# Two-layer convolution and local attention on 8 images: the position map kept in DRAM, the emptying of the queries moved, and inverse roots by Ln and Exp

## The chip, the cores and the metric

The kernel runs on one core of a Trainium2 chip. The metric is the device time of one execution in microseconds (us). A core has TensorE (PE in the profile) for matmuls, VectorE (DVE), ScalarE (ACT) and GpSimd (POOL) for the rest, and SyncE (SP), which here only issues DMAs. "PEld" is TensorE's loading of weights, listed apart from the matmuls. "SPq" and "ACTq" are DMA issues by these two engines.

## The reference

Eight images of 256 channels and 64 x 64 pixels, in float32, go through two residual layers. Both begin with a group norm over 32 groups of 8 channels. Cut to what matters:

```python
def layer0(x):                       # x is group-normed
    x1, x2, x3 = conv1x1(x, w1), conv1x1(x, w2), conv1x1(x, w3)   # 32, 32, 256 channels
    h = concat(x1, unfold3x3(reflect_pad(x2)))                    # 320 channels
    h = relu(bn(h)); h = relu(bn(conv1x1(h, cw1)))                # 32 channels
    w = conv1x1(h, cw2) + cb2                                     # 9 weights per pixel and group
    return sum over the 9 taps of unfold3x3(zero_pad(x3)) * w

def layer1(x):                       # x is group-normed
    pe = Wp @ position(64, 64) + bp  # the position map: depends on neither the image nor x
    q, k, v = conv1x1(x, Wq) * 64 ** -0.5, conv1x1(x, Wk), conv1x1(x, Wv)     # 4 heads of 64
    att = softmax over 7x7 neighbours of q . unfold7x7(reflect_pad(k) + reflect_pad(pe))
    out_att = sum over neighbours of att * unfold7x7(reflect_pad(v))
    wts = softmax over 9 branches of conv1x1(x, Wfc)
    hid = relu(depthwise3x3(x, w1))  # one per branch, with the branch's own kernels
    out_conv = sum over branches of depthwise3x3(hid, w2) * wts
    return rate1 * out_att + rate2 * out_conv

x = x + layer0(group_norm(x))
x = x + layer1(group_norm(x))
```

`group_norm` divides by sqrt(variance + eps); this inverse root is one of the things the change rewrites.

## The kernel before

**Tiling.** An image is cut into NB = 8 bands of R = 8 rows (512 pixels). Channels lie on the 128 partitions, in two tiles (`ct` = 0, 1). The main loop (line 1032) counts bands with `g`, from -12 to 63; `b, i = divmod(g, 8)` are image and band. Layer 1 of band `g` is worked on while layer 0 of band `g + 12` is prepared beside it, because layer 1's group norm needs the whole of layer 0's image first. In the loop's first 12 rounds layer 0 runs alone ("alone" in the code). A band has STEPS = 8 steps (`s`): four pairs of 8 x 8 query tiles for each `ct`, `m` = 0 to 3.

**One step.** Scores go from TensorE (L736, `sco`) to DVE, which adds the mask and takes the negated maximum (L750, `nmax`). ACT takes the exponentials and sums them (L758, `prob` and `tot`). DVE inverts `tot` (L765) and ACT scales (L767). One step later TensorE transposes the probabilities (L773, `ptp`), ACT copies them out (L775), and TensorE multiplies them with the values (L785). Beside this stand, in each step, two matmul groups of the branch weights (L872, `pf`, four 128x512 matmuls with their weights), each with an exponential on ACT (L877, `ex`), the depthwise convolutions on DVE (L829, L855), the sum over the branches on POOL and DVE (L1087, L885 to L899), and the taps of layer 0: TensorE makes their weights (L464, `pw`), DVE multiplies (L477, `prod`), POOL adds up (L485, `xg`).

**Order of work.** The whole order is written out by hand: nothing is reordered, and each engine executes its instructions in the order in which the Python code emits them. `advance()` ends a place in this order, and `after(n, f)` runs `f` n places later. `beside(g, s)` gives three lists of extra work for a step: `head`, `mid`, `end`. A function in `head` or `mid` issues its matmuls when called and may return a second function, called one place later, which empties PSUM. `steer` adds the loads and the group norms. The order around `head` is:

```python
prob, nmax = masked(nm, m, sco)
...
    tot = exponentials(nm, prob, nmax)
ahead = [f() for f in head]
advance()
for f in ahead:
    if f:
        f()
```

**What the change touches.**

- *Queries* (L662 to L677): two matmuls per `ct` into `pq`, and at once, in the same function, an ACTIVATE that writes the scaled result into `qb` (L674). In most bands the queries stand in `mid`. In an image's first band the second half stands in `head` of step 3 and in its last band too, and the first half of such a band in `head` of step 7 of the band before. There ACT's `qb` comes behind the exponentials of the same step. `keys` in `head` of step 7 of other bands return their emptying as a second function, so their order stays.
- *Position map* (L643 to L652): for the rows of keys that are new in a band, POOL adds a column vector `pecol` and a row vector `perow` into one tile `pe` with a single buffer. It is called from `mid` in step 5 of the band before, or in step 4 if the coming band is an image's first or last. The first band of an image has 11 new rows (352 KB), the middle ones 8 (256 KB), the last 5 (160 KB). Its readers are DVE's `keys` (L700 and L707), which add it to the keys in `kb`. POOL also copies the six old rows of `kb` (L660).
- *Inverse roots* in `gn_affine` (L225 to L272), with `sc_a` for layer 0's norm and `sc_b` for layer 1's: two small matmuls `pg` (L237) form means over groups, then come variance plus eps (L258, DVE), square root (L262, ACT), reciprocal (L266, DVE), spread over fixed numbers of places. `rstd_` (L143 to L146) does the same once for the two batch norms. ACT's functions stand in table sets, and a change of the set is an instruction of its own (ACT_TABLE_LOAD); the compiler inserts it, at the line of the ACTIVATE that needs it.

**Queues.** SP issues nearly all DMAs, in order: a DMA that waits for something holds all later ones. For a band it issues the stores of the values `vd` (L614, L618, L625), the loads of value tiles `vt` (L636), the rows of layer 1's input `yp` (L557 to L561), the residual `xr` (L1000), and for layer 0 `xc`, `xs`, `xg`, `x3q` and the stores of `x` (L376, L523). ACT normalises `yp` in place (L566) when it has landed. The constants are loaded by ACT's queue at the start (L109).

**PSUM.** The pool tag "gen" has four buffers, which `pq`, `pk`, `pf`, `pw`, `ptp`, `pv` (L594), `p3` (`p` in the profile, L369), `pg` and others share in turn. A matmul group therefore starts only when the group four before it has been emptied, and TensorE's waits are named after whichever engine empties late.

Of the kernel before, what the change touches and what calls it, by code (L numbers as in the profile page):

```python
# [10 lines left out]
F32 = mybir.dt.float32  # L11
BF16 = mybir.dt.bfloat16
AF = mybir.ActivationFunctionType
# [5 lines left out]
P = 128  # L19
# [36 lines left out]
CHUNK = R * KW  # L56
NPROB = 2 * CHUNK
NEG = -1.0e30


AHEAD = NB + 4
# [25 lines left out]
def conv_layers_kernel(ctx: ExitStack, tc: tile.TileContext, ins: dict, out: bass.AP):  # L87
    nc = tc.nc
# [18 lines left out]
    def load(name, shape, src=None, now=True):  # L107
        t = const.tile(shape, F32, name=f"c_{name}")
        late.append(lambda: nc.scalar.dma_start(out=t, in_=ins[name] if src is None else src))  # L109
        if now:  # L110
            late.pop()()
        return t

    gmat = load("gmat", [P, P])
    par = load("par", [P, NPAR])
    chan = load("chan", [P, NCT, NCHAN], ins["chan"].rearrange("(t p) n -> p t n", p=P))
# [23 lines left out]
    for t in probs + x3n + h2n:  # L140
        nc.gpsimd.memset(t, 0.0)

    def rstd_(out_, var, eps):  # L143
        nc.vector.tensor_scalar(out_, var, eps, None, ALU.add)
        nc.scalar.activation(out_, out_, AF.Sqrt)
        nc.vector.reciprocal(out_, out_)  # L146


    bn1s = const.tile([P, 3], F32, name="bn1s")
# [34 lines left out]
    dram = ctx.enter_context(tc.tile_pool(name="dram", bufs=3 * NB, space=DRAM))  # L184
# [40 lines left out]
    def gn_affine(sts, means, name, done):  # L225


        n = len(sts)
        mv = stat.tile([P, n, 2], F32, name=f"mv_{name}", tag=f"mv{n}")
        for ct, st in enumerate(sts):  # L230
            nc.vector.bn_aggr(mv[:, ct, :], st)
        mean, var = mv[:, :, 0], mv[:, :, 1]
        gm, d, sc, bi = (stat.tile([P, n], F32, name=f"{v}_{name}", tag=f"{v}{n}") for v in ("gm", "d", "sc", "bi"))

        def group_means(v, k):
            pg = ps.tile([P, n], F32, name=f"pg_{name}_{k}", tag="gen", bufs=4)
            nc.tensor.matmul(pg, means, v, start=True, stop=True)  # L237
            return pg


        def a1():
            pg = group_means(mean, 0)
            after(2, lambda: a2(pg))

        def a2(pg):
            nc.vector.tensor_copy(gm, pg)
            for ct in range(n):
                c = slice(ct, ct + 1)
                nc.vector.tensor_scalar(d[:, c], pg[:, c], mean[:, c], None, ALU.subtract)
                nc.vector.tensor_scalar(d[:, c], d[:, c], d[:, c], var[:, c], ALU.mult, ALU.add)  # L250
            after(5, a3)

        def a3():
            pg = group_means(d, 1)
            after(2, lambda: a4(pg))

        def a4(pg):
            nc.vector.tensor_scalar(sc, pg, GN_EPS, None, ALU.add)  # L258
            after(2, a5)

        def a5():
            nc.scalar.activation(sc, sc, AF.Sqrt)  # L262
            after(4, a6)

        def a6():
            nc.vector.reciprocal(sc, sc)  # L266
            for ct in range(n):
                c = slice(ct, ct + 1)
                nc.vector.tensor_scalar(bi[:, c], gm[:, c], sc[:, c], -1.0, ALU.mult, ALU.mult)
            done(sc, bi)  # L270

        after(3, a1)  # L272
# [370 lines left out]
    def position(b, i):  # L643

        first, last = new_keys(i)
        n, a = last - first, i * R + first
        pe = images[b].pe[i] = w1.tile([P, KW - PAD, W], F32, tag="pe", name=f"pe_{b}_{i}", bufs=1)
        nc.gpsimd.tensor_add(
            pe[:, :n],
            pecol.unsqueeze(1).to_broadcast([P, n, W]),  # L650
            perow[:, a : a + n].unsqueeze(2).to_broadcast([P, n, W]),
        )  # L652

    def key_block(b, i, ct):

# [354 lines left out]
    with tc.manual_schedule():  # L1010

        for i, use in enumerate(("xc", "xc", "xr", "xr", "xs", None, None, None)):
            t = None
            if use is None:
                t = w1.tile([P, NCT, RP, W], F32, tag="yp", name=f"x_{i}", bufs=3)
                t = t.rearrange("p t r c -> p t (r c)")[:, :, :BAND]
            x = first_stats(0, i, use, t)
            if use == "xc":
                images[0].xc[i] = x
            advance()  # L1020
        for r in range(NB, AHEAD0 - AHEAD):
            first_stats(*divmod(r, NB))
        for _ in range(10):
            advance()
        scaled_weights(0)
        for _ in range(32):
            advance()
        for n, f in enumerate(layer1_loads()):
            after(4 * STEPS * (3 + n), f)

        pending, before, conv, convs = [], None, None, []
        for g in range(-AHEAD, B * NB):
            b, i = divmod(g, NB)
            for s in range(STEPS):
                ct, m = divmod(s, NT // 2)
                head, mid, end = beside(g, s)
                steer(g, s)
                if g >= 0:
                    nm = f"{b}_{i}_{ct}_{m}"
                    weighted = []  # L1040
                    if m % 2 == 0:
                        sco = score_tile(nm)
                        for e in range(2):
                            scores(b, i, ct, m + e, sco)
                        small = small_tile(nm)
                        weighted, pending = weigh_steps(pending, small), []
                        if s == 0 and g + AHEAD < B * NB:
                            mid.append(small_maps(*divmod(g + AHEAD, NB), small))
                        if s in (4, 6) and convs:
                            convs.pop()(small)  # L1050
                        if before is not None:
                            pending.append((before[:-1], transposed(nm, before[-1])))
                    prob, nmax = masked(nm, m, sco)
                    for a, po in weighted:
                        add_values(*a, po)
                    tot = exponentials(nm, prob, nmax)
                ahead = [f() for f in head]
                advance()
                for f in ahead:
                    if f:  # L1060
                        f()
                if g >= 0:
                    ex, exb = w1.tile([P, 2, BAND], F32, tag="ex", name=f"ex_{nm}", bufs=3), ex if m else None
                    branch_weights(b, i, ct, m, 0, ex)
                    if m % 2:
                        pending.append((before[:-1], transposed(nm, before[-1])))
                    if m in (0, 2):
                        todo = list(conv[0])
                    for _ in range(2):
                        todo.pop(0)()  # L1070
                advance()
                if g >= 0:
                    probabilities(prob, tot)
                rest = [f() for f in mid]
                advance()
                for f in rest:
                    if f:
                        f()
                if g >= 0:
                    for _ in range(2 if m % 2 == 0 else len(todo)):  # L1080
                        todo.pop(0)()
                    before = (b, i, ct, m, prob)
                advance()
                if g >= 0:
                    branch_weights(b, i, ct, m, 1, ex)
                    if exb is not None:
                        after(4, lambda ex=ex, exb=exb: nc.gpsimd.tensor_add(ex, ex, exb))  # L1087
                    if m == 1:
                        conv[1]()
                        conv = depthwise_middle(b, i, ct)  # L1090
                    if m == NT // 2 - 1:
                        oc = depthwise_end(b, i, ct, conv[1])
                        after(4, lambda a=(b, i, ct, ex, oc): dynamic_sum(*a))
                if s % 4 == 3 and 0 <= (g * NCT + ct + 1) < B * NB * NCT:
                    gn, cn = divmod(g * NCT + ct + 1, NCT)
                    conv = depthwise_begin(*divmod(gn, NB), cn)
                advance()
                for f in end:
                    f()
                advance()  # L1100
        for last in (before, None):
            for a, po in weigh_steps(pending, small_tile(f"end{last is None}")):
                add_values(*a, po)
            pending = [] if last is None else [(last[:-1], transposed("end", last[-1]))]
        for _ in range(40):
            advance()
# [84 lines left out]
```

## Time and profile before

| | us |
|---|---|
| median of three runs | 3909.05 (3906.9 to 3915.44) |
| the profiled execution | 3911.49 |
| its span | 3909.7 |
| waits of ACT for `nmax`, 203 of them, in all | 224.3 |
| waits of ACT for `pq`, 19 of them, in all | 7.0 |
| POOL's `pe`, one | 0.72, 1.04 or 1.37 |
| ACT_TABLE_LOAD, one | 1.283 |
| `qb` (L674), one | 0.667 |

The mean clock granted to TensorE was 0.994 of full speed. The page has 24620 matmuls and 6779 instructions of ACT. Of the table loads 13 stand at L262 (in front of a square root) and the one at L758 is the first for an exponential:

```profile
L262 ACT ACT_TABLE_LOAD  x13: 1283/1283/1283, 451.5 to 3435.1; - x13
L262 ACT ACTIVATE sc_a<-sc_a x8: 189/204/204, 24.5 to 2808.0; 128x2 f32<-128x2 f32 x8
L262 ACT ACTIVATE sc_b<-sc_b x8: 185/202/204, 202.1 to 3436.4; 128x1 f32<-128x1 f32 x8
```

In this view of one line of the kernel, a row is an operation with its count, then the shortest, median and longest duration in ns, then the start of the first and the last in us. Times in a timeline are start and length. A bracket such as [0.75 <-ACT ex L877] says that the engine stood idle for 0.75 us before the instruction, and that the event that ended it was ACT's work at line 877 on tile `ex` (for a PSUM tile of the shared pool: the emptying of a buffer).

### The profile page before, as it was taken

What the parts mean: (1) busy time and instruction counts of PE and PEld (TensorE: products, weight loads), DVE (VectorE), ACT (ScalarE), POOL (GpSimd) and SP (SyncE); (2) the same over time, 40 slices, a digit from 0 to 9 for tenths busy, and PEclk for the clock granted to TensorE, in tenths of its full rate; (3) what the DMA queues carried; (4) which work ended last, traced back from release to release, by engine and by line L of the source; (5) the groups of instructions that cost most, each with busy time, mean ns of one, the idle gap of its engine ahead of it and who ended that gap; (6) DMA issues with size and microseconds to landing.
All of it is one profiled execution on the core that took longest, in us unless ns stands there. A gap on an engine that the chain in (4) does not pass through costs nothing.

```text
span 3909.7 us, 71679 instructions
## 1 busy us (share of the span) xinstructions
PE 3778.1 (97%) x24620; PEld 2112.2 (54%) x24620; DVE 3419.7 (87%) x7143; ACT 2835.8 (73%) x6779; POOL 3172.5 (81%) x2156
## 2 busy tenths in 40 slices
PE   5889999999999999999999999999999999999998
PEld 2445555555555555555555555555555555555554
DVE  6879898899898999899998998989988889978778
ACT  4457777777777777777777777777777777677776
POOL 4768888888887988888888888978988888956665
PEclk9999999999999999999999999999999999999999
DMA  8764443543444543543444443444433443322221
GB/s 245 208 168 128 127 118 115 143 121 116 124 123 123 142 118 105 140 131 114 139 111 128 136 119 113 127 138 116 130 111 100 133 122 94 87 85 79 72 60 35
DMA packets 429710, 473.36 MB, mean 121 GB/s; under 512 B 60992, under 2 KB 322208, under 8 KB 429088
## 3 DMA queue, kind: packets, MB, share of 16 engines
q1 hardware_dynamic: 412768, 453.01, 41.1%
q10 hardware_dynamic: 16576, 15.76, 1.3%
q8 instruction: 194, 3.18, 0.3%
q14 instruction: 172, 1.41, 0.1%
HBM read 329.08 MB, written 143.00 MB: 121 GB/s over the span
## 4 chain that ended last, share of the span: by engine, by line
PE 41%; DVE 24%; POOL 15%; ACT 11%; issue 6%; DMA 3%; SPq 0%; ACTq 0%; POOLq 0%; DVEq 0%
PE pf L872 19%; POOL xg L485 8%; DVE prod L477 7%; DVE acc L855 5%; DVE rec L893 5%; POOL ex L1087 4%; PE small L785 3%; PE pv L594 3%; ACT x L343 3%; PE ptp L773 3%; PE sco L736 3%; PE pk L692 2%; PE pq L670 2%; ACT ex L877 2%; DMA x<-x3n 2%
## 5 line engine op out<-in xcount | busy, mean ns | idle before, releaser
L872 PE MATMUL pf<-yp,c_wfc 128*128 128x512 f32 x4096 | 1916.6, 594 | 17.8 <-ACT ex L877 6.8
L485 POOL TENSOR_TENSOR xg<-xg,prod 128x1024 f32<-128x1024 f32 x549 | 1198.8, 2184 | 106.7 <-DVE prod L477 82.5
L872 PEld LDWEIGHTS pf<-yp,c_wfc 128*128 128x128 f32 x4096 | 738.5, 190 | 719.0 <-issue 629.2
L1087 POOL TENSOR_TENSOR ex<-ex,ex 128x1024 f32<-128x1024 f32 x384 | 908.2, 2365 | 66.4 <-ACT ex L877 62.5
L829 DVE SCALAR_TENSOR_TENSOR acc<-yp,c_chan,acc 128x504 f32<-128x504 f32 (+3 forms) x1104 | 775.4, 702 | 64.7 <-ACT acc L820 41.3
L477 DVE SCALAR_TENSOR_TENSOR prod<-pw,c_par,x3q 128x1040 f32<-128x1040 f32 x576 | 737.0, 1286 | 103.6 <-PE pw L464 57.4
L855 DVE SCALAR_TENSOR_TENSOR acc<-hid,c_chan,acc 128x504 f32<-128x504 f32 (+3 forms) x1024 | 750.6, 733 | 18.1
L877 ACT ACTIVATE ex<-pf 128x512 f32<-128x512 f32 x1024 | 602.0, 588 | 214.5 <-PE pf L872 197.5
L758 ACT ACTIVATE prob<-prob,nmax 128x196 f32<-128x196 f32 x1024 | 459.1, 451 | 224.5 <-DVE nmax L750 224.3
L767 ACT ACTIVATE prob<-prob,tot 128x196 f32<-128x196 f32 x1024 | 413.1, 452 | 249.5 <-DVE tot L765 248.3
L894 POOL TENSOR_TENSOR tot<-tot,rec 128x256 f32<-128x256 f32 x254 | 185.4, 730 | 398.0 <-DVE rec L893 391.6
L893 DVE RECIPROCAL rec<-tot 128x256 f32<-128x256 f32 x256 | 445.8, 1742 | 9.5 <-POOL tot L894 4.3
L775 ACT COPY pt<-ptp 112x512 f32<-112x512 f32 x511 | 295.0, 577 | 110.3 <-PE ptp L773 109.9
L750 DVE CUSTOM_DVE_ANT_0 prob<-sco,c_mask 128x196 f32<-128x196 f32 x1024 | 324.4, 354 | 28.1 <-PE sco L736 28.0
L773 PEld LDWEIGHTS ptp<-ident,prob 128*112 128x112 f32 x2044 | 227.2, 133 | 184.2 <-issue 157.1
L773 PE MATMUL ptp<-ident,prob 128*112 128x128 f32 x2044 | 319.0, 279 | 0.0
L785 PEld LDWEIGHTS small<-pt,vt 112*64 112x64 f32 x8144 | 258.2, 137 | 77.4 <-issue 75.7
L785 PE MATMUL small<-pt,vt 112*64 112x64 f32 x8144 | 293.7, 225 | 1.2 <-DMA vt<-vd 1.2
L369 PE MATMUL p<-xc,w3s 128*128 128x512 f32 x512 | 248.3, 608 | 15.8 <-ACT ex L877 15.8
L594 PE MATMUL pv<-c_wv,yp 128*128 128x256 f32 x1056 | 252.1, 381 | 7.4 <-ACT qb L674 6.0
L888 POOL TENSOR_SCALAR tot<-tot 128x512 f32<-128x512 f32 x127 | 243.6, 1918 | 11.1
L464 PEld LDWEIGHTS pw<-h2n,c_c 128*128 128x128 f32 x1152 | 176.2, 192 | 137.6 <-issue 122.7
(139 smaller groups left out, 4750.0 us busy)
## 6 DMA issues: line engine op xcount, KB each, us to landing
vt<-vd SPq DMA_DIRECT2D x512, 112.0 KB
x3q<-x SPq DMA_DIRECT2D x128, 264.0 KB
xc<-in_x SPq DMA_DIRECT2D x64, 512.0 KB
xg<-in_xg SPq DMA_DIRECT2D x64, 512.0 KB
yp<-x SPq DMA_DIRECT2D x128, 256.0 KB
xr<-x SPq DMA_DIRECT2D x64, 512.0 KB
out_x<-xr SPq DMA_DIRECT2D x64, 512.0 KB
xs<-in_x SPq DMA_DIRECT2D x57, 512.0 KB
```

The costliest lines, as they stand in the source:

```text
L477: nc.vector.scalar_tensor_tensor(prod[:, :, :RUN], pw[:, j, :RUN].unsqueeze(1).to_broadcast([P, SHARE, RUN]), par[:, PCB2 + k : PCB2 + k + 1],
L485: nc.gpsimd.tensor_add(im.xg[i], im.xg[i], rows(prod))
L758: nc.scalar.activation(prob[:, h, :NKEY], prob[:, h, :NKEY], AF.Exp, bias=nmax[:, h : h + 1], scale=-1.0, accum_out=tot[:, h : h + 1],)
L767: nc.scalar.activation(prob[:, h, :NKEY], prob[:, h, :NKEY], AF.Copy, scale=tot[:, h : h + 1])
L773: nc.tensor.transpose(ptp[:, h, ch], prob[:, h, ch * CHUNK : (ch + 1) * CHUNK], ident)
L785: nc.tensor.matmul(po[half[h], :, t * TQ : (t + 1) * TQ], im.vt[i + ch, m][:n, t, (2 * ct + h) * HD : (2 * ct + h + 1) * HD], pt[:n, h, ch ...
L829: nc.vector.scalar_tensor_tensor(o, yp[:, ct, ra + dr : rb + dr, ca + dc : cb + dc], chan[:, ct, CW1 + k : CW1 + k + 1], o, ALU.mult, ALU.add,
L855: nc.vector.scalar_tensor_tensor(o, hid[:, ra + dr : rb + dr, ca + dc : cb + dc], chan[:, ct, CW2 + k : CW2 + k + 1], o, ALU.mult, ALU.add,)
L872: nc.tensor.matmul(pf, wfc[:, kt, 2 * m + j, ct * P : (ct + 1) * P], images[b].yp[i][:, kt, PAD : PAD + R], start=(kt == 0), stop=(kt == N ...
L877: nc.scalar.activation(ex[:, j].rearrange("p (r c) -> p r c", r=R), pf, AF.Exp)
L893: nc.vector.reciprocal(rec, v)
L1087: after(4, lambda ex=ex, exb=exb: nc.gpsimd.tensor_add(ex, ex, exb))
```

## The change

Three things are changed.

1. One table set, which has both the logarithm and the exponential, is loaded at the kernel's start, ahead of the constants. An inverse root is now Ln and then Exp with scale -0.5, both in place on ACT; the square root and DVE's reciprocal are gone. The places in the written order stay (the function `a5` issues both ACTIVATEs).
2. `position` lets POOL compute `pe` only for image 0. SP then stores each band's map into a DRAM tile of its own (`kept[i]`), and for the other seven images SP loads it from there, at the place where POOL's addition was.
3. In the main loop the `head` functions, with the queries and their ACTIVATE of `qb`, are called ahead of `exponentials`, not behind.

```diff
+TABLES = "natural_log_exp_and_others"
...
+    nc.scalar.preload_act_table_set(TABLES)
     gmat = load("gmat", [P, P])
...
+    def inverse_root(v):
+        nc.scalar.activation(v, v, AF.Ln)
+        nc.scalar.activation(v, v, AF.Exp, scale=-0.5)
+
     def rstd_(out_, var, eps):
         nc.vector.tensor_scalar(out_, var, eps, None, ALU.add)
-        nc.scalar.activation(out_, out_, AF.Sqrt)
-        nc.vector.reciprocal(out_, out_)
+        inverse_root(out_)
...
         def a5():
-            nc.scalar.activation(sc, sc, AF.Sqrt)
+            inverse_root(sc)
             after(4, a6)

         def a6():
-            nc.vector.reciprocal(sc, sc)
             for ct in range(n):
...
         pe = images[b].pe[i] = w1.tile([P, KW - PAD, W], F32, tag="pe", name=f"pe_{b}_{i}", bufs=1)
+        if b:
+            nc.sync.dma_start(out=pe[:, :n], in_=kept[i])
+            return
         nc.gpsimd.tensor_add(
             pe[:, :n],
             pecol.unsqueeze(1).to_broadcast([P, n, W]),
             perow[:, a : a + n].unsqueeze(2).to_broadcast([P, n, W]),
         )
+        kept[i] = dram.tile([P, n, W], F32, tag=f"pe{i}", name=f"pe_{i}", bufs=1)
+        nc.sync.dma_start(out=kept[i], in_=pe[:, :n])
+
+    kept = {}
...
+                ahead = [f() for f in head]
+                if g >= 0:
                     tot = exponentials(nm, prob, nmax)
-                ahead = [f() for f in head]
                 advance()
```

## The prediction

> **What bounds the kernel now.** I read the busy times first, then the same times by stretch, then who waited for whom on TensorE within one image, and last the timeline around each of those waits.
>
> ```profile
> PE 3778.1 (97%) x24620; PEld 2112.2 (54%) x24620; DVE 3419.7 (87%) x7143; ACT 2835.8 (73%) x6779; POOL 3172.5 (81%) x2156
> ```
>
> ```profile
> 230.00:3410.00 3180.00, 3122.40 (x20618) 1757.71 (x20617) 2846.73 (x5981) 2377.23 (x5700) 2720.67 (x1824) 1.00 0.44 123
> 3410.00:3910.00 500.00, 486.78 (x3187) 267.06 (x3185) 402.00 (x950) 358.20 (x896) 304.49 (x208) 0.99 0.21 66
> ```
>
> The columns of the second view are stretch, length, then busy time of PE, PEld, DVE, ACT, POOL, the clock, the DMA share and GB/s. From 230 us on TensorE idles 57.6 us in 3180, and in the last 500 us hardly outside the final microseconds. Its 128x512 matmuls follow each other every 0.43 us (0.19 for the weights, 0.24 until the next), so it streams. Whatever the change frees on ACT, DVE or POOL is worth at most what TensorE waits for them. The images repeat every 471 us; in the fourth (1641 to 2112) TensorE is busy 463.14 us, and these are its waits but for three of 0.8 us together (total, times, longest):
>
> ```profile
> PE p L369 <- ACT ex L877: 2.2, 8, 0.4
> PE pf L872 <- DVE prod L477: 1.1, 1, 1.1
> PE pv L594 <- ACT qb L674: 1.0, 1, 1.0
> PE pg_a L237 <- ACT ex L877: 0.8, 1, 0.8
> PE pf L872 <- ACT ex L877: 0.8, 1, 0.8
> PE sco L736 <- DVE kb L707: 0.7, 4, 0.2
> ...
> PE sco L736 <- POOL oc L898: 0.3, 1, 0.3
> ...
> ```
>
> So of 7.8 us an image, three single waits make 2.9, and each stands beside something that the change edits:
>
> ```profile
> 2042.81 1.28 ACT L877 ACT_TABLE_LOAD   x1
> ...
> 2046.11 1.98 PE L872 MATMUL pf<-yp,c_wfc 128*128 128x512 f32 x4 [0.75 <-ACT ex L877]
> ...
> 2088.53 0.67 ACT L674 ACTIVATE qb<-pq,bq 128x512 f32<-128x512 f32 x1
> ...
> 2089.25 1.99 PE L594 MATMUL pv<-c_wv,yp 128*128 128x256 f32 x8 [0.99 <-ACT qb L674]
> ...
> 2106.16 1.37 POOL L648 TENSOR_TENSOR pe<-pecol,perow 128x704 f32<-128x704 f32 x1
> ...
> 2107.49 4.44 POOL L485 TENSOR_TENSOR xg<-xg,prod 128x1024 f32<-128x1024 f32 x2
> ...
> 2109.70 1.30 DVE L477 SCALAR_TENSOR_TENSOR prod<-pw,c_par,x3q 128x1040 f32<-128x1040 f32 x1 [1.08 <-POOL xg L485]
> ...
> 2111.06 1.98 PE L872 MATMUL pf<-yp,c_wfc 128*128 128x512 f32 x4 [1.12 <-DVE prod L477]
> ```
>
> **What the Trainium skill says.** "ScalarE: Activation LUTs", section "What ACT_TABLE_LOAD costs", prices a change of set at 1.283 us for the load plus 1.38 us of drain, and its section on table sets names a set with both exp and ln. The trace agrees with the load (1.283 us, 28 of them) but shows no drain: the ACTIVATE before ends within 0.02 us of the load, the next starts at once. I use 1.283. "Perfetto Trace Analysis", section "Identifying the Most-Contended Engine", warns that TensorE's busy time says little; here the even 0.43 us spacing says that it is full. "DMA: Bandwidth & Descriptors", section "Anatomy of one DMA", gives 2.0 us plus bytes at 436 GB/s: an estimate of 2.6 us for 256 KB. In this trace the last of six yp loads was issued at 256.84 and its reader ran at 259.17, 2.3 us later. "PSUM — Partial Sum Buffer", section "Engine vs sequencer instructions", calls the ACT, DVE and POOL queues strict FIFO; the trace's chains show the same, and it is why a moved instruction counts.
>
> **The change part by part.**
>
> *Inverse roots.* 28 table loads become one: 27 x 1.283 = 34.6 us off ACT; 18 roots gain one ACTIVATE each (0.2 us, the row of L262; 3.6 us) and lose a reciprocal on DVE (0.16 us). ACT is busy 73%, so most of it shrinks idle time. On the path are the sc_b roots: ACT's pf evacuation (L877) comes late and TensorE stands 0.75 us, in six images: -4.5 us. Within 8 us behind the loads at the sc_a roots TensorE has no wait: 0. The first load for exp, at 238.54, precedes a TensorE wait of 1.94 us at 246.39, but ACT then waits 5.53 us for yp at 259.17 anyway: 0. The preload now stands ahead of nine constant loads that ACT issues. SP's early loads waited 1.9 and 4.1 us on c_gmat and c_rowp, so it costs between 0 and 1.3 us; ACT's queue issues DMAs beside running ACTIVATEs (24.94 and 24.95), so I take 0.
>
> *Queries.* The order of instructions, built without a run, has TensorE's stream unchanged and on ACT 31 exchanges: qb (0.67 us) now precedes two exponentials (1.3 us). At 2087.64 ACT had idled 1.49 us for DVE's nmax while pq had ended at about 2085.2; so qb fits into that idle time, the exponentials keep their time, and the 0.99 wait ends. At the other places (1648.75, 1681.27, 2060.82) the idle time before the exponentials is 0.72 to 1.31 us; only at the first does pq end as late as nmax, and the exponentials slip by 0.6 us, ahead of a DVE reciprocal that nothing waits for. Smaller waits on qb of 0.21 us, six times: -1.3 us; one of 1.03 us at 268.88: -1.0.
>
> *Position map.* Per image POOL loses 1.37 + 6 x 1.04 + 0.72 = 8.3 us, 58 us in seven. Where POOL has slack this is nothing. At an image's end it has none: it is busy 7.8 to 7.9 of every 8 us from 2081 to 2112, and pe lies ahead of the two xg sums for which DVE and then TensorE wait. Without it they start 1.37 us sooner. The 0.99 (queries) and 1.12 lie 22 us apart before the same POOL end, so together they yield not 2.11 but POOL's 1.37, less 0.02 for DVE's reciprocal in between: six ends x 1.35 = -8.1 us. (The seventh falls where TensorE is full.) POOL's kb copies behind pe come sooner too, ending the 0.29 us waits named after oc: of six, 1.2 us.
>
> *What it adds.* 56 loads of 352, 256 or 160 KB on SP's queue (14.7 MB, 3% more traffic), each waiting for DVE's last reader of the single pe buffer. In an ordinary band that reader ends at 1742.1, SP comes to the load at about 1748.5, the first reader of the new map runs at 1768.4: 20 us for a 2.6 us transfer. SP's next work waits until 1757 anyway: 0. And eight stores in the first image hold SP until POOL has made the map. SP reaches the first at 223.77, while POOL ends pe at 227.86:
>
> ```profile
> 223.77 1.30 SPq L614 DMA_DIRECT2D vd<-vc  x2
> ...
> 226.49 1.37 POOL L648 TENSOR_TENSOR pe<-pecol,perow 128x704 f32<-128x704 f32 x1
> ...
> 254.46 0.44 SPq L557 DMA_DIRECT2D yp<-x  x1
> ...
> 259.17 1.13 ACT L566 ACTIVATE yp<-yp,aff 128x896 f32<-128x896 f32 x1 [5.53 <-DMA yp<-x]
> ```
>
> Held for 4.1 us are vd's stores, xr, x3q, the vt loads and yp, for which ACT waits already. SP's pauses until there (0.8 at 238.9, 0.8 at 250.5) can absorb 1.6, so +2.5 to +4.1; with the 352 KB store ahead of vd at the 245 GB/s of the first slice, 1.5 more. I take +3.3; from 0 to 5.6 for the range. The next six hold SP 5.8 us (343.90 to 349.7) ahead of vd, vt and yp; 3.05 us of pause follows at once, and yp, issued at 361.15, is used at 373.7: 0. The eighth holds it 14 us (622 to 636.4) and pushes yp from 652.6 to about 658, for use at 665.1: 0, with some 2 us to spare.
>
> **Sum.** -4.5 - 1.3 - 1.0 - 8.1 - 1.2 + 3.3 = -12.8 us. The profiled execution took 3911.49 us, its span 3909.7; on it the sum gives 3898.7. The median of the three runs, 3909.05, lies 2.4 below; there it gives 3896. What ends next is ACT at a band's start, the eight short waits of p on ex, which stay.
>
> **The rivals.** *All the named waits go* (also DVE's kb, 5.2 us in all, because DVE waits less for POOL; queries and map add up to 2.11 at each end; the hold costs nothing): 12.7 + 4.5 + 2.3 + 1.8 + 5.2 = 26.5, 3882.5. For it: DVE waits 4.6 us an image for POOL's xg. Against: the shared POOL end. *The gains are lost again*: TensorE runs ahead and waits longer for ACT, which is busy 7.84 to 7.97 of 8 us from 1657 to 1673 and again from 2065 to 2081. If a third survives, -5.4 + 3.3: 3907. Against it: ACT idles before these stretches, so they can begin sooner. *Slower*: SP's hold, in the first image only. If it reaches yp and vt in each band past the pauses, 4.1 + 1.5 + 6 x 2.75 + 5.2 = 27 us against 16.1 gained: 3920. It decides where yp lands more than about 7 us later than now. Against it: 12 us from issue to use in an ordinary band. *The change doesn't do what it says*: the built order shows one table load and 56 loads for 56 sums, so I give it nothing.
>
> **How the numbers follow.** Forecast 0.58; all waits go 0.12; gains lost 0.23; slower 0.07. About 0.2% (7.8 us) is what a measurement of this kernel tells from no change. The first two lie under 3901.2: faster 0.70, same 0.23, slower 0.07. The range, 3883 to 3907, runs from the first rival to the second.
>
> **What would show it.** Right: one table load; no TensorE wait at qb or behind the sc_b root; the wait on prod at an image's end under 0.2 us; TensorE idle under 6 us an image; yp in the first band later by 2 to 5 us. Wrong: DVE's kb waiting for a DMA; ACT's yp waiting in bands 1 to 7; the waits of p on ex growing by what the others lose.

## The result, and the profile after

The changed kernel took 3901.7 us (median of 13 runs, 3896.4 to 3903.81), the kernel before 3909.05 us (13 runs beside them, 3903.39 to 3915.44). The ratio is 0.9978, 95% interval 0.9970 to 0.9985: 8.6 us faster by the ratio, 6 to 12 by its interval. The profiled execution took 3901.4 us, its span 3899.5. The medians lie 7.35 us apart, about the 7.8 us that the prediction took for the least that such a measurement tells from no change; the interval of the ratio leaves out 1. The busy times of the page, and the long stretch (columns as in the prediction):

```profile
PE 3774.0 (97%) x24620; PEld 2112.0 (54%) x24620; DVE 3415.8 (88%) x7125; ACT 2809.8 (72%) x6770; POOL 3118.1 (80%) x2100
```

```profile
230.00:3410.00 3180.00, 3129.03 (x20685) 1762.65 (x20684) 2852.42 (x5983) 2362.49 (x5712) 2678.06 (x1781) 1.00 0.46 127
```

POOL lost 54 us of work, ACT 26, and in the long stretch TensorE's idle time fell from 57.6 us to 51.0. The waits of TensorE within the fourth image (1637 to 2106; total, times, longest), without the later rows:

```profile
PE p L373 <- ACT ex L888: 1.7, 8, 0.4
PE pf L883 <- ACT ex L888: 1.3, 2, 0.7
PE pg_a L242 <- ACT ex L888: 1.1, 1, 1.1
PE pf L883 <- DVE prod L481: 1.0, 1, 1.0
```

Of the three waits that the prediction marked, only `qb`'s is gone. The one on `prod` at the image's end stands as before (1.0 for 1.1), and the one of `pf` on `ex` behind the inverse root too (0.73 us at 2042.31; the second in that row, 0.55 us, is new, in step 5 of the image's first band). In the run's first band a wait has grown; the first timeline is the kernel before, the second the changed kernel:

```profile
251.62 0.61 PE L464 MATMUL pw<-h2n,c_c 128*128 128x132 f32 x4
...
254.23 0.45 PE L785 MATMUL small<-pt,vt 112*64 112x64 f32 x8 [0.88 <-DMA vt<-vd]
```

```profile
247.37 0.61 PE L468 MATMUL pw<-h2n,c_c 128*128 128x132 f32 x4
...
255.78 0.70 PE L796 MATMUL small<-pt,vt 112*64 112x64 f32 x8 [6.67 <-DMA vt<-vd]
```

TensorE came 4.25 us sooner to this place (1.56 of them because the first `pf` of this trace started sooner, at 235.32 for 236.88) and left it 1.55 us later, because the value tiles `vt` were not there.

**Where the gain lies.** Both programs have the same 4096 branch matmuls (`pf`) in the same order, so the start of the k-th in one trace can be set against the k-th in the other. Counted from the first `pf` of band 1 in one image to that in the next, an image took 471.05 us before and 468.93 after (mean of the five from image 1 to image 6). Within an image, the lead of the new trace grows mostly at the last band. In the fourth image it is 4.16 us at the start of that band and 5.67 at the end of its step 3; in the first band of the fifth image it is 6.12 at the end of step 3 and back to 5.50 at the end of step 5. A second trace of the changed kernel gives 469.09 for the 468.93, so differences of some 0.2 us an image are at the limit of this measure. I call it "the period" below.

### The profile page after: what moved, and what is told of

It is laid out like the page before. It is cut to its first block, busy times and chain, and to the rows that moved or that the text cites. A ratio compares the mean times of both kernels' runs of the same rounds, so it can differ in the third digit from the quotient of the medians.

```text
span 3899.5 us, 71759 instructions
## 1 busy us (share of the span) xinstructions
PE 3774.0 (97%) x24620; PEld 2112.0 (54%) x24620; DVE 3415.8 (88%) x7125; ACT 2809.8 (72%) x6770; POOL 3118.1 (80%) x2100
## 4 chain that ended last, share of the span: by engine, by line
PE 38%; POOL 22%; DVE 20%; ACT 10%; issue 5%; DMA 4%; SPq 0%; ACTq 0%; POOLq 0%; DVEq 0%
PE pf L883 18%; POOL xg L489 10%; POOL ex L1099 7%; DVE prod L481 6%; DVE rec L904 4%; DVE acc L866 4%; PE small L796 3%; ACT x L347 3%; PE pv L598 3%; PE ptp L784 3%; PE sco L747 3%; PE pq L681 2%; PE pk L703 2%; DMA x<-x3n 2%; ACT ex L888 2%
```

## The experiments

Times are medians; the ratio is to the kernel before on the same chip, with its 95% interval. "First band" is the time from the first `pf` matmul of the run to the second group of step 5: 47.09 us before, 50.54 after. Period and first band come from one trace each.

| run | time, us | ratio | period, us | first band, us |
|---|---|---|---|---|
| inverse roots alone | 3910.36 | 1.0005 (0.9997 to 1.0013) | 471.01 | 48.04 |
| queries alone | 3912.16 | 1.0007 (0.9999 to 1.0015) | 471.03 | 46.34 |
| map alone | 3903.47 | 0.9981 (0.9975 to 0.9988) | 468.99 | 50.87 |
| changed kernel, late stores | 3898.81 | 0.9972 (0.9961 to 0.9982) | 468.99 | 48.13 |
| changed kernel again | 3903.64 | 0.9981 (0.9974 to 0.9988) | 469.09 | 50.88 |
| map alone, late stores | 3900.1 | 0.9975 (0.9966 to 0.9984) | 469.16 | 47.22 |
| late stores, moved copy | 3896.86 | 0.9966 (0.9954 to 0.9978) | 468.60 | 49.00 |
| map alone, late stores, moved copy | 3901.0 | 0.9975 (0.9966 to 0.9985) | 469.08 | 47.23 |
| late stores, moved copy, nmax first | 3894.02 | 0.9959 (0.9945 to 0.9973) | 468.16 | 48.08 |
| late stores, moved copy, one sum left out | 3888.02, one run | | 468.45 | 46.90 |
| late stores, moved copy, nmax first, one sum left out | 3888.63, one run | | 467.22 | 47.24 |
| the row above, with the square roots of before | 3899.43, one run | | 469.14 | 46.55 |

(Rows that do not say "alone" start from the changed kernel.)

### One part of the change at a time

Each of the first three kernels is the kernel before with one of the three parts of the change: roots, order of the queries, map.

> The kernel before with the inverse roots alone changed. Theory: at the sc_b root ACT's late emptying of pf is set by DVE's nmax, which ended at 2044.53 just as ACT was free (2044.59); so the TensorE wait there stays at 0.7 to 0.8 us and the period of an image stays 471.0 to 471.1 us. Gain only ahead of the second step of the first band, 3 to 4.5 us, as no store holds SP: about 3905 in all. Rival (my prediction's step): ACT's table loads make the wait, it goes to under 0.1 us, the period falls by 0.75 us to 470.3 and the time by 4.5 us more, to about 3900.

> The kernel before with the order of queries and exponentials alone changed. Theory: the wait of pv on qb (0.99) and the wait of pf on prod at the image's end (1.12) stand before one POOL end, so the first goes and the second grows to about 2.1 to 2.4; the 0.21 wait on qb in the first band comes back as one on ex of about 0.5. Period 470.7 to 471.1 us, time within 2 us of before apart from 1 us in the first image. Rival: each wait is its own; prod's stays at 1.1, the period falls by 1.2 to 469.8, time about 3900.

> The kernel before with the position map alone changed. Theory: POOL's end of an image comes 1.35 us sooner; the wait on prod goes from 1.12 to under 0.2 while pv's wait on qb stays at 1.0, and the 0.29 wait behind POOL's copy of kb goes: period 469.5 to 469.8 us. The first image gets 1.5 to 4 us longer by the stores on SP. Time about 3902 to 3904. Rival: POOL's 1.37 us are worth nothing without the queries (something else than POOL's end holds prod): prod's wait stays over 0.8, period 470.6 or more, time about 3910.

On the waits and on who has the gain the theory held for all three; two of its figures missed. The roots alone were to gain 3 to 4.5 us in the first band, for a time of about 3905 us; the time stayed (3910.36) and the first band became longer (48.04 us for 47.09). And the map's period fell below the 469.5 to 469.8 expected. The sum is lopsided: the map alone has the whole period gain (2.06 of 2.12 us), the other two have none. The waits of the queries' kernel in its fourth image, from 1635 to 2106, and of the map's, from 1638 to 2108, each without the later rows:

```profile
PE pf L872 <- DVE prod L477: 4.8, 2, 2.4
PE p L369 <- ACT ex L877: 2.6, 8, 0.8
PE pf L872 <- ACT ex L877: 1.3, 2, 0.8
```

```profile
PE p L369 <- ACT ex L884: 1.7, 8, 0.4
PE pv L594 <- ACT qb L681: 1.0, 1, 1.0
PE pg_a L237 <- ACT ex L884: 0.8, 1, 0.8
PE pf L879 <- ACT ex L884: 0.8, 1, 0.8
```

With the queries alone `qb` is in no row, but the wait on `prod` is 2.4 us long, for 1.1 before (the stretch has two of these because it takes in two image ends). TensorE comes sooner to the image's end and waits there for the same POOL work: in the kernel before, POOL sets the end. With the map alone it is the other way round: `prod` is in no row and `qb`'s 1.0 stays. In the changed kernel `qb`'s wait is gone and `prod`'s is there (1.05). So with POOL's sum away the two ends lie close together, and either wait takes the place of the other.

The roots' kernel shows what stood behind the table loads. ACT beside the sc_b root:

```profile
2037.45 0.19 ACT L146 ACTIVATE sc_b<-sc_b 128x1 f32<-128x1 f32 x1
2037.68 0.20 ACT L147 ACTIVATE sc_b<-sc_b 128x1 f32<-128x1 f32 x1
...
2040.06 0.60 ACT L881 ACTIVATE ex<-pf 128x512 f32<-128x512 f32 x1 [0.68 <-PE pf L876]
2042.18 0.46 ACT L762 ACTIVATE prob<-prob,nmax 128x196 f32<-128x196 f32 x1 [1.52 <-DVE nmax L754]
```

In place of the two loads, 2.57 us together, there are 0.68 + 1.52 = 2.20 us of idle time (and the second ACTIVATE of the root takes 0.2 more): ACT is free sooner and then waits for `nmax`. TensorE's wait behind it is 0.73 us for 0.75.

### The stores on SP

```diff
-        nc.sync.dma_start(out=kept[i], in_=pe[:, :n])
+        after(28, lambda: nc.sync.dma_start(out=kept[i], in_=pe[:, :n]))
```

> The changed kernel, with the eight stores of the map issued 28 places later, behind the next band's loads, so that SP doesn't wait for POOL. Theory: the hold of SP makes TensorE's wait for vt in the first band (6.67 us); it falls to 1.5 to 3.5 us, and the first band ends 3 to 5 us sooner: about 3898 in all, period unchanged at 468.9. Rival: TensorE only arrives sooner and vt would land then anyway (its landing is set by the DMAs themselves): the wait stays at 5 us or more and the time at 3901 to 3902.

> The changed kernel again, for a second trace and a comparison within one call. Expected: the same period of 468.8 to 469.0 us; the start of the first band's first branch weights moves by up to 4 us either way (it differed by 6.6 us between kernels that share that part); time 3900 to 3903.

> The position map alone, with its stores 28 places later; queries and inverse roots as before. Theory: the map alone makes the whole steady gain and the queries and roots add nothing, so period 469.0 us and time within 2 us of the changed kernel with late stores (3898.8): 3897 to 3901. Rival: queries and roots are worth their own 2 to 5 us beside the map: 3901 to 3904.

SP's own waits, up to the first `vt` loads, show the hold: first before, where SP came free when `vc` was ready, then the changed kernel (each wait counts all the time that SP stands there, in the second also what it would have waited for `vc`).

```profile
SPq L614 <- ACT vc L601: 7.7, 1, 7.7
```

```profile
SPq L661 <- POOL pe L655: 16.0, 1, 16.0
```

And TensorE's wait for the value tiles between 230 and 290 us, with the map alone and then with its stores late:

```profile
PE small L792 <- DMA vt<-vd: 7.1, 2, 6.3
```

```profile
PE small L792 <- DMA vt<-vd: 1.2, 2, 1.0
```

The changed kernel again came out slightly above what was expected (469.09 us, 3903.64). With late stores and the whole change the longest wait for `vt` fell from 6.67 us (7.45 in the second trace) to 3.67, and the first band from 50.54 (50.88) to 48.13 us: the hold costs 2.4 to 2.8 us with the whole change, and 50.87 - 47.22 = 3.65 us with the map alone, where it goes entirely (47.22 for 47.09 before). With the whole change that is less than the 3 to 5 us expected, because the rival has a part too: with the roots alone, and no store at all, TensorE waited 4.58 us for `vt`. In the kernel before, the first load of a table for an exponential stood ahead of a wait of 1.94 us; without it that wait is 0.94, TensorE comes sooner to `vt`, and waits there. In medians, with late stores the map alone took 3900.1 us and the whole change 3898.81, on different chips, with ratios 0.9975 and 0.9972: a difference that these intervals do not resolve. The periods, 469.16 and 468.99, leave the other two parts at most about 0.2 us an image beside the map.

### What ends an image: POOL and the queries together

```diff
             if i:
-                nc.gpsimd.tensor_copy(kb[:, : 2 * PAD], im.kb[i - 1, ct][:, R:])
+                copy = nc.scalar.copy if i == NB - 1 and ct else nc.gpsimd.tensor_copy
+                copy(kb[:, : 2 * PAD], im.kb[i - 1, ct][:, R:])
```

> The changed kernel with late stores, and with one of POOL's copies of old keys (0.52 us, second channel tile of an image's last band) moved to ACT. Theory: POOL's chain sets the image's end and TensorE waits 1.05 us for it, so POOL's 0.52 us come off the wait on prod (to about 0.5) and off the period: 468.4 us, some 3 us in six images: 3895 to 3897. Rival: DVE, idle only 0.5 us before that prod, or ACT with the copy ahead of qb, takes its place: prod's wait or one on qb makes up for it, period 468.8 to 469.2, time 3898 to 3900.

> The position map alone with late stores and the moved copy; queries and inverse roots as before. Theory: without the exchange TensorE waits for qb (0.98 us) and not for POOL, so POOL's 0.52 us are worth nothing: period 468.9 to 469.2, prod's wait under 0.1, qb's at 1.0; 3897 to 3901. Rival: the copy is worth its 0.5 us an image here too, period 468.5, 3895 to 3897.

Both came out as the theory said, within 0.2 us of its periods. One copy less on POOL (0.52 us) takes the wait on `prod` from 1.07 to 0.60 us and the period from 468.99 to 468.60 where the queries are early, and leaves 469.08 for 469.16 where they are late and `qb` (0.98 us) is what TensorE waits for. So the order of the queries is worth at most 0.2 us an image in the change as it stands, and becomes worth something (469.08 - 468.60 = 0.48 us) when POOL gets shorter still.

### Three reasons for one wait

```diff
-PRODUCTS_AT = ((1, 2),) * 5, ((7, 14, 10), (9, 17, 13), (12, 20, 16))
+PRODUCTS_AT = ((1, 2),) * 3 + ((2, 3), (1, 2)), ((7, 14, 10), (9, 17, 13), (12, 20, 16))
```

> The changed kernel with late stores, the moved copy, and in each band's step 5 DVE's nmax ahead of the first prod of that step (the two prods of that step one place later). Theory: the waits of pf on ex behind the sc_b root (0.74 us) and in the first band's step 5 (0.55 us) were set by DVE's nmax standing behind a prod, not by table loads or by qb; both fall under 0.1 us, the period from 468.55 to 467.2 to 467.6 us, time 3889 to 3893. Rival: the prods, 0.8 us later, hold their PSUM buffer or POOL's xg, and a wait of pf on prod of 0.5 us or more takes the place; period 468.5 or more, time 3896 or more.

Half of it held, and the time (3894.02) and the period (468.16) stayed above the expected ranges. The 0.55 us in step 5 of the first band are gone: what the new order of the queries saved at `qb` had been lost again behind DVE, which in the changed kernel is busy for 7.93 of the 8 us from 1684 to 1692. At the sc_b root 0.65 us stayed. The timeline there:

```profile
2035.33 2.36 POOL L1100 TENSOR_TENSOR ex<-ex,ex 128x1024 f32<-128x1024 f32 x1
...
2037.72 0.60 ACT L889 ACTIVATE ex<-pf 128x512 f32<-128x512 f32 x1 [1.43 <-PE pgc L546]
...
2038.37 1.13 PE L884 MATMUL pf<-yp,c_wfc 128*128 128x512 f32 x2 [0.65 <-ACT ex L889]
```

The exponentials are now early (2035.31), yet ACT stands still until 2037.72. The profile names TensorE's `pgc`, but ACT does not read it. POOL's sum of `ex` ends at 2037.69, 0.03 us ahead: it frees one of three `ex` buffers, and by the order of the buffers ACT writes into that one. To test this, the next kernels leave the sum out in the band concerned (`i` = 6, `ct` = 0, `m` = 3):

```diff
-                    if exb is not None:
+                    if exb is not None and (i, ct, m) != (NB - 2, 0, 3):
```

> The kernel with nmax first, with one of POOL's sums of ex left out (2.37 us, in the seventh band of each image, first channel tile, last step), so a part of the dynamic branch's sum is missing there. Theory: with nmax early, ACT's emptying of pf behind the sc_b root waits for the third ex buffer, which this sum frees; without it the TensorE wait there (0.65 us) falls under 0.1 us. Rival: it is ACT or TensorE itself (pgc), and the wait stays at 0.5 to 0.7 us.

> The same sum of ex left out, but nmax behind the prod as in the changed kernel (late stores, moved copy). Theory: DVE's nmax alone makes the wait behind the sc_b root, so it stays at 0.6 to 0.75 us. Rival: the sum was the only cause, and the wait falls under 0.2 us.

> As the first of these three (nmax first, one sum of ex left out in each image's seventh band), but with the square roots and their table loads of the kernel before. Theory: the two table loads, 2.57 us on ACT, hid behind nmax and the sum; with both away they show as a TensorE wait of 0.5 to 0.8 us at the sc_b root, and the other waits are as in the first. Rival: the loads are in ACT's idle time and the wait is under 0.2 us.

With `nmax` early and the sum left out the wait is gone (period 467.22 us). With the sum left out and `nmax` late it is 0.73. With `nmax` early, the sum left out and the square roots back, it is 0.75 again:

```profile
2037.42 1.28 ACT L885 ACT_TABLE_LOAD   x1
2038.71 0.60 ACT L885 ACTIVATE ex<-pf 128x512 f32<-128x512 f32 x1
...
2040.09 0.58 ACT L885 ACTIVATE ex<-pf 128x512 f32<-128x512 f32 x1
```

So table loads, `nmax` and POOL's sum each hold the same wait at 0.65 to 0.75 us, and taking away one of them, or two, gives at most 0.1 us here. With the other two gone, the loads are worth 469.14 - 467.22 = 1.9 us an image (one trace each), of which 0.75 stand here and 0.64 behind the loads of the sc_a root (the other 0.5 were not traced). The times of these three runs say nothing on a complete kernel, since part of the work is missing.

Of the complete kernels the one with late stores, the moved copy and `nmax` first is the best seen: 3894.02 us, ratio 0.9959 (0.9945 to 0.9973), against 0.9978 and 0.9981 for the changed kernel. Its interval overlaps that of the first at its edge only, and not that of the second.

## Why the prediction was right, and where it was not

The time lies in the range and on the forecast side; of the forecast 12.8 us the medians show 7.35. What held is the step with the largest share, POOL's end of the image. That the total came as near as it did is in part luck: steps worth 6.8 us yielded nothing, and the map yielded 3.1 us more than was counted for it.

- *Map and queries at the image's end, -8.1 us: the size was right, the share wrong.* One POOL end, 1.35 us sooner, is what came: TensorE's lead grew from 4.42 (step 1 of the last band) to 5.74 at the wait on `prod`. The step put this down to the two parts together. The map alone has nearly all of it (1.26 us, at the wait on `prod`); the queries alone have none. And the list of what would show the step right was wrong by the step's own sum: if two waits of 2.11 us yield 1.35, then 0.76 has to stay, and on `prod` 1.05 did.
- *POOL's copies of `kb`, -1.2 us: right or a little low.* The wait of 0.29 us is gone, and TensorE's lead grows by 0.36 there. Two waits of `p` on `ex` in each image fell from 0.44 to 0.18 us, in the map's kernel too, with 0.25 us of lead each. These two were not forecast, and what shortens them was not traced.
- *Inverse roots behind sc_b, -4.5 us: wrong, worth 0.* The step read a wait from what stood last before it. The trace of before shows two other reasons close behind:

```profile
2042.94 2.37 POOL L1087 TENSOR_TENSOR ex<-ex,ex 128x1024 f32<-128x1024 f32 x1
...
2044.45 0.08 DVE L750 DVE_READ_ACCUMULATOR2_ANT nmax<- 128x1 f32 x1
...
2044.59 0.45 ACT L758 ACTIVATE prob<-prob,nmax 128x196 f32<-128x196 f32 x1
...
2045.48 0.58 ACT L877 ACTIVATE ex<-pf 128x512 f32<-128x512 f32 x1
```

DVE's first `nmax` was finished at 2044.45 + 0.08 = 2044.53, 0.06 us ahead of the exponential at 2044.59 that the table loads had delayed, and POOL's sum ended at 2042.94 + 2.37 = 2045.31, 0.17 us ahead of the `ex` that TensorE waited for. So no more than about 0.06 us was to be gained, and 0.02 came (0.73 for 0.75).
- *Small waits on `qb`, -1.3 us: wrong, worth 0.* All six went and came back two steps later as waits on `ex`. The forecast slip of the exponentials did not come either (0.03 us behind `nmax`); DVE, which the step did not look at, is full there. *The 1.03 us at 268.88*, -1.0: went the same way, a lead of 1.2 us gained there and given back at step 5.
- *SP's hold, +3.3 us: right* (2.4 to 3.65), with its place mistaken in part: what TensorE itself waited for were the value tiles `vt`. ACT's wait for `yp`, which the step named, grew too, from 5.53 us to 11.65; `yp` was issued 3.0 us later, counted from the first `pf` (1.5 by the clock, at 255.92). The later stores cost nothing, as forecast. Against the kernel with late stores, and beyond the first band's 2.4 us, those of bands 1 to 6 delayed SP's next `vd` by 5.2 to 6.9 us (5.8 forecast) and the eighth by 12.5 (14). Behind the eighth ACT waited 0.82 us for `yp` in one trace of the changed kernel and not in the other. Yet from the end of the first-band measure to band 1 of the second image the changed kernel takes 488.84 us with them and 488.80 without the hold.
- *Loads of the map and the preload, 0: right as far as seen.* The preload was not tested by itself. DVE's `kb` waits for `pk` only, and TensorE's waits on `kb` stay at 5.2 us in all.

On the pair of profiled executions, 10.1 us apart, the sum without the two wrong steps and the 1.0 is -8.1 - 1.2 + 3.3 = -6.0. The map's period gain is 2.06 us where 1.55 was counted for its parts (the other 0.5 are the two waits of `p`), which over six images is 3.1 more; the rest is within what the start of a run scatters. The rival "the gains are lost again" holds for two of the three edits, by DVE and POOL rather than by ACT. Of the signs that the prediction named for itself, the single table load, the end of the wait on `qb` and the later `yp` came; the waits behind the sc_b root and on `prod` stayed, and TensorE idles 469 - 462.54 = 6.46 us in the fourth image, not under 6.

"PSUM — Partial Sum Buffer", section "Engine vs sequencer instructions", of the Trainium skill calls the queues of ScalarE, VectorE and GpSimd strict FIFO; the largest step that came out rests on that order, POOL's sums behind `pe`. For SP, which that section does not name, the traces show it: with the store SP issued the values `vd` at 225.06, right behind the store at 224.64, and with late stores at 220.07. "ScalarE: Activation LUTs", section "What ACT_TABLE_LOAD costs", gave a price for the load that the trace shows (1.283 us); of its drain of 1.38 us the traces show nothing, the gap ahead of a load is at most 0.02 us. The mistake was to take a price for a gain.

## What to carry to other kernels

A wait is worth removing only by as much as the next reason for it lies earlier: before counting it, look on every engine for what else ended within some tenths of a microsecond of it (the mask's maximum, a buffer that a third engine frees), and price the edit by the second latest. Where two waits stand ahead of one shared end, they are one gain, and it belongs to whatever shortens that end. In these runs the store placed in SP's ordered queue cost by what it waited for, not by its bytes (2.4 to 3.65 us, and nothing that could be seen when issued later): issue it where its data are long ready.

## What the runs showed of the hardware

The first `pf` matmul started between 229.31 and 237.33 us in the thirteen traces of the changed kernel and the experiments, among them 230.28 (queries alone) and 237.33 (map alone, late stores), two kernels whose code differs only behind that point, and 235.32 and 232.07 in two executions of the very same program. On one chip it was 237.33 and 233.29 for the map alone with late stores, without and with the moved copy, which again differ only behind it. So the beginning, where the DMAs are 76% busy, scatters by some microseconds (why was not tested), while the period of an image was the same within 0.2 us in two executions of the changed kernel. In this kernel a gain of a few microseconds is read better from the position of one instruction in two traces than from a median of runs.
